# Four layers, two streams of emission: lower weights for the steps of layer 1's first two passes

## The chip, the cores and the metric

The kernel runs on one NeuronCore of a Trainium2 chip, as one program. The metric is the device time of one execution in microseconds; lower is better. The times before are those of three runs. The profile is of one further execution.

## The reference, cut to what matters

Input x has 4 images of 48 channels and 256 x 256 pixels, in float32. Four layers follow one another, each of the form x = x + layer(group_norm(x)). The group norm (`_gn`) takes mean and variance over a whole image, so a layer of an image can start only when the layer before it has finished the last row of that image. Images don't depend on one another.

```python
# layer 0: 1x1 conv to 288 channels, 3x3 depthwise, split into q, k, v;
#          8x8 patches: irfft2(rfft2(q) * rfft2(k)), normalised over channels, times v, 1x1 conv
x = x + _L0_conv_ref(_gn(x), ...)
# layer 1: 1x1 conv to 288 channels, 8x8 patches filtered in frequency,
#          3x3 depthwise, gelu(first half) * second half, 1x1 conv
x = x + _L1_conv_ref(_gn(x), ...)
# layer 2: integral image of gn(x); two 3x3 convs give a box and a scale for each pixel;
#          the integral image is sampled bilinearly at the box's four corners: (A + D - B - C) / area
x = x + _L2_conv_ref(_gn(x), ...)
# layer 3: 1x1 conv to 192, 3x3 depthwise, gelu gate, 1x1 conv, 8x8 frequency filter
x = x + _L3_conv_ref(_gn(x), ...)
```

## The kernel before

**Two streams of emission.** The program is written by two streams of Python generators, `run` (L1278). Stream a has layer 0 and layer 1 of image 0, then of image 1, 2 and 3, and after these layer 3 of images 0 to 3. Stream b has the statistics of the inputs and the filter matrices of layer 1 (`patch_weights`), and then layer 2 of images 0 to 3. Each generator emits a piece of its layer and yields a number, the weight of the step. `advance` adds it to its stream's counter `at`, and the stream with the lower counter emits next. A layer waits for the one below it of the same image: its stream's counter is then raised to the counter at which that one was done. So the weights decide only which instructions of stream b stand between which of stream a; no instruction depends on them. Every engine then takes its own instructions in the order emitted.

**The layers and their weights.** Layer 0 (L466) goes in units of two rows, 128 and 7 to drain, with two yields of 7 for each (L606, L616): 1890. Layer 1 (L659) has three passes, with pools of their own:

- Pass A (L660 to L710): 16 strips of rows are normalised (L684), multiplied by `win` (L697, 32 matmuls a strip), copied from PSUM by VectorE and ScalarE (L702, L704) and stored to `hD` in DRAM. It yields twice a strip.
- Pass B (L711 to L789): 72 groups of four channels. `fetch` loads `hg` from `hD` and the matrices `ct`, `tt` and `ht`; `filtered` (L728) applies the frequency filter, neighbours' edges are copied by DMA into `yh`, and `gated` (L741, L742) the depthwise convolution and the gate; the result goes to `gD` in DRAM. It yields once a group, 73 times.
- Pass C (L790 to L845): `gs` is loaded from `gD`, turned, projected to 48 channels, added to x and stored. It yields 5 each of 64 times.

Layer 2 (L912) begins with `sums` (L848), which builds the integral image as a table in DRAM: for both halves twelve yields of 7 and eight of 10, 328 in all. Two yields of 30 start its main part, which has 32 pieces with four steps each and a drain of four: every step has two yields of 11. A step issues 16 gathers on POOL's queue (`gather`, L1037) into `V`, which has 3 buffers; then `add` multiplies and adds the gathered corners of the step before on VectorE (L1048, L1050, L1051), `convolve` (L947), `project` (L966, L971) and `boxes` (L982 to L1029) prepare a piece two ahead, and `finish` (L1062, L1069) adds the result to x. Layer 2 weighs 3292 in all.

Layer 3 (L1134) has 128 units and 7 to drain with two yields of 4: 1080. Layers 0 and 3 share `convolve2` (L427, L435).

**Queues.** Stream a issues its DMAs from SP, stream b from POOL. Layer 2's columns A and B come through ACT's queue (L301 to L305), and `sums` stores its table from SP (L909). The two streams have PSUM banks of their own (5 for a, 2 for b) and take SBUF from opposite ends.

Of the kernel before, what the change touches and what calls it, by code (L numbers as in the profile page):

```python
# [188 lines left out]
class Net:  # L189
# [469 lines left out]
    def layer1(self, x, mr, y):  # L659
# [4 lines left out]
        with ExitStack() as ctx:  # L664
            w = ctx.enter_context(self.pool("wa", 1))
            sb = ctx.enter_context(self.pool("ba", 2))

            win = w.tile([112, 288], F32, name="win")
            mh = w.tile([112, 2], F32, name="mh")
            xns = [w.tile([112, 2, PW], F32, name=self.nm("xn")) for _ in range(2)]  # L670
            xps = [w.tile([112, 16, 128], F32, name=self.nm("xp")) for _ in range(2)]
            for t in xns:
                nc.vector.memset(t[32:64], 0.0)
            nc.vector.memset(mh[32:64], 0.0)
            for h in range(2):
                self.dma(win[64 * h : 64 * h + 48], a["L1_w_in"])
                self.dma(mh[64 * h : 64 * h + 48], mr[48 * h : 48 * h + 48])

            def normalise(s):

                for r in range(0, 8, 2):
                    xn = xns[r // 2 % 2]
                    self.load_rows(xn, x, 8 * s + r, 2, 64)
                    nc.vector.tensor_scalar(  # L684
                        xps[s % 2][:].rearrange("p b (r c) -> p r b c", c=16)[:, r : r + 2],
                        xn[:, :, 1:257].rearrange("p r (b c) -> p r b c", c=16),
                        mh[:, 0:1], mh[:, 1:2], ALU.subtract, ALU.mult,
                    )

            normalise(0)  # L690
            for s in range(NS):
                xp = xps[s % 2]
                hs = sb.tile([128, 4 * NG, 2, 16], F32, name="hs", tag="hs")
                for b in range(16):
                    for h in range(2):
                        ps = self.bank()
                        nc.tensor.matmul(  # L697
                            ps[:, :288], xp[64 * h : 64 * h + 48, b, :], win[64 * h : 64 * h + 48],
                            start=True, stop=True,
                        )  # L700
                        if h:
                            nc.vector.tensor_copy(hs[:, :, h, b], ps[:, :288])  # L702
                        else:
                            nc.scalar.copy(hs[:, :, h, b], ps[:, :288])  # L704
                    if b == 7:
                        if s + 1 < NS:
                            normalise(s + 1)
                        yield 13
                self.dma(hD[:, :, s, :], hs[:].rearrange("p (g c) h b -> p g (c h b)", c=4))
                yield 13  # L710
        with ExitStack() as ctx:  # L711
            w = ctx.enter_context(self.pool("wb", 1))
            sb = ctx.enter_context(self.pool("bb", 2))
            ys = [w.tile([128, YL], F32, name=self.nm("ys")) for _ in range(2)]
            yhs = [w.tile([NZ, YL], F32, name=self.nm("yh")) for _ in range(2)]
            hts = [w.tile([NZ, 4, 128], F32, name=self.nm("ht")) for _ in range(3)]
            for t in ys + yhs + hts:
                nc.vector.memset(t[:], 0.0)

            pick = lambda t, k, c: t[:k, Y0 + YC * c : Y0 + YC * c + 32 * YW].rearrange(  # L720
                "p (h s b) -> p s h b", h=2, b=YW
            )[:, :, :, :16]
            order = lambda t: t.rearrange("p (s h b) -> p s h b", h=2, b=16)
            todo, gt = None, None

            def filtered(c):
                ps = self.bank()
                nc.tensor.matmul(  # L728
                    ps[:].rearrange("p (s n) -> p s n", n=32), ct[:, c, :], hg[:, :, c, :], start=True, stop=True
                )  # L730
                if c % 2:
                    nc.vector.tensor_copy(pick(yt, 128, c), order(ps[:]))  # L732
                else:
                    nc.scalar.copy(pick(yt, 128, c), order(ps[:]))

            def gated(c):
                go, yo, yho, to, ho = todo
                both = []
                for q in (c, c + 2):
                    ps = self.bank()  # L740
                    nc.tensor.matmul(order(ps[:]), to[:, q, :], pick(yo, 128, q), start=True, stop=False)  # L741
                    nc.tensor.matmul(order(ps[:]), ho[:, q, :], pick(yho, NZ, q), start=False, stop=True)  # L742
                    both.append(ps)
                gl = sb.tile([128, 512], F32, name="gl", tag="gl")
                nc.scalar.activation(gl[:], both[0][:], AF.Gelu)
                nc.vector.tensor_mul(  # L746
                    gt[:, :, 2 * (go % 2) + c, :], gl[:].rearrange("p (s n) -> p s n", n=32),
                    both[1][:].rearrange("p (s n) -> p s n", n=32),
                )


            def fetch(g):
                hg = sb.tile([128, NS, 4, 32], F32, name="hg", tag="hg")
                self.dma(hg[:].rearrange("p s c n -> p s (c n)"), hD[:, g])
                ct = sb.tile([128, 4, 128], F32, name="ct", tag="ct")
                self.dma(ct[:], self.cD[g])
                tt = sb.tile([128, 4, 128], F32, name="tt", tag="tt", bufs=3)
                ht = hts[g % 3]
                tv = self.tD[4 * g : 4 * g + 4].rearrange("c (k m) -> k c m", m=128)
                self.dma(tt[:], tv[:128])  # L760
                self.dma(ht[:NH], tv[128:])
                return hg, ct, tt, ht

            fetched = {0: fetch(0)}
            for g in range(NG + 1):
                if g < NG:
                    yt = ys[g % 2]
                    if g + 1 < NG:
                        fetched[g + 1] = fetch(g + 1)
                    hg, ct, tt, ht = fetched.pop(g)  # L770
                if todo is not None and todo[0] % 2 == 0:
                    gt = sb.tile([128, NS, 4, 32], F32, name="gt", tag="gt")
                for c in range(2):
                    if g < NG:
                        filtered(2 * c)
                        filtered(2 * c + 1)
                    if todo is not None:
                        gated(c)
                if g < NG:
                    yh = yhs[g % 2]  # L780
                    n = YL - 2 * Y0
                    for k, m, p0, dp, far in AROUND:
                        self.dma(
                            yh[k : k + m, Y0 : Y0 + n], yt[p0 : p0 + (m - 1) * dp + 1 : dp, Y0 + far : Y0 + far + n]
                        )
                if todo is not None and todo[0] % 2:
                    self.dma(gD[:, :, todo[0] // 2, :], gt[:].rearrange("p s c n -> p s (c n)"))
                todo = (g, yt, yh, tt, ht)
                yield 12  # L789
        st = self.stat.tile([CP, 129, 6], F32, name=self.nm("st"), tag="st" + self.stream, bufs=1)  # L790
        with ExitStack() as ctx:
            w = ctx.enter_context(self.pool("wc", 1))
# [579 lines left out]
```

## Time and profile before

| | us |
|---|---|
| median of 3 runs | 20884.65 |
| lowest and highest | 20843.57, 20913.25 |
| profiled execution: its own time | 20882.08 |
| profiled execution: span of the instructions | 20880.3 |

| engine | busy us | share of the span |
|---|---|---|
| PE matmul | 18892.3 | 90% |
| PE weight load | 12001.4 | 57% |
| VectorE (DVE) | 10763.0 | 52% |
| ScalarE (ACT) | 5909.3 | 28% |
| GpSimd (POOL) | 8637.2 | 41% |

The DMA engines move 3440 MB at a mean of 165 GB/s. The granted clock of TensorE is 0.922 on the mean. Busy shares are averages over stages with different limits. The profile's slices and the windows by stage show where each engine is full. A count in brackets, as x1360, is the number of instructions in a stretch. Matmuls are pipelined and each of these float32 matmuls appears as two records.

### The profile page before, as it was taken

The numbers are of one execution on the slowest core, as the hardware profiler recorded it, in microseconds if no ns is written. First come the engines' busy times: TensorE is split into PE (matmuls) and PEld (weight loads), VectorE is DVE, ScalarE is ACT, GpSimd is POOL, SyncE is SP. The second block draws the span as 40 slices with busy tenths as digits, with TensorE's granted clock in tenths as the row PEclk, the third lists the DMA queues.
The fourth block names the chain that finished last, engine by engine and source line by source line (L and its number), as shares of the span: only waits on it lengthen the run. The fifth ranks groups of instructions, "written<-read, shape, count | busy, mean of one in ns | idle before, by whom it ended". The sixth has DMA issues, their size and how long they took to land.

```text
span 20880.3 us, 231985 instructions
## 1 busy us (share of the span) xinstructions
PE 18892.3 (90%) x79032; PEld 12001.4 (57%) x79032; DVE 10763.0 (52%) x21931; ACT 5909.3 (28%) x12275; POOL 8637.2 (41%) x8887
## 2 busy tenths in 40 slices
PE   7998798999878989998788899997888999999999
PEld 4565435666533346665433466654334787878888
DVE  4544322477765534677645447776554255555521
ACT  2333312344321123443311234433112211111111
POOL 1000000277754511777555216775552066666600
PEclk9899799999968999999689899996899999999999
DMA  4623886555588975555889755558897566666633
GB/s 114 135 55 82 233 217 194 137 132 134 132 235 230 241 207 139 130 134 127 233 230 240 219 133 130 133 127 229 236 239 225 137 150 151 158 152 160 151 76 74
DMA packets 2444896, 3440.27 MB, mean 165 GB/s; under 512 B 580102, under 2 KB 1997038, under 8 KB 2333179
## 3 DMA queue, kind: packets, MB, share of 16 engines
q1 hardware_dynamic: 1908216, 2084.50, 38.2%
q0 software_dynamic: 452560, 1110.45, 21.1%
q10 hardware_dynamic: 82944, 230.48, 4.4%
q8 instruction: 635, 10.40, 0.2%
q14 instruction: 541, 4.43, 0.1%
HBM read 2486.99 MB, written 802.77 MB: 158 GB/s over the span
## 4 chain that ended last, share of the span: by engine, by line
PE 65%; DMA 15%; DVE 7%; POOL 7%; issue 4%; SPq 1%; ACT 1%; DVEq 0%; ACTq 0%; POOLq 0%
PE ps L427 19%; POOL V L1037 7%; PE ps L947 6%; PE ps L728 5%; PE ps L435 4%; PE ps L741 4%; DMA ct<-cD 4%; PE ps L742 3%; PE ps L697 3%; PE ps L828 3%; DMA hD<-hs 2%; PE ps L1188 2%; DVE V L1050 2%; PE ps L815 1%; PE ps L966 1%
## 5 line engine op out<-in xcount | busy, mean ns | idle before, releaser
L1037 POOL DMA_INDIRECT V<-t,idx x8192 | 8227.0, 1004 | 4897.9 <-issue 2346.8
L427 PE MATMUL ps<-W,A 128*128 128x288 f32 (+1 forms) x24576 | 5547.3, 374 | 85.9 <-DMA A<-x 23.4
L427 PEld LDWEIGHTS ps<-W,A 128*128 128x128 f32 x24576 | 4281.6, 191 | 1226.6 <-issue 523.4
L227 POOL DMA_DIRECT2D X<-x x192 | 144.5, 757 | 4302.6 <-DMA x<-xt 3040.1
L1050 DVE TENSOR_TENSOR V<-V 128x1536 f32<-128x1536 f32 (+3 forms) x2048 | 1839.3, 900 | 19.2
L1048 DVE TENSOR_TENSOR V<-V,w 128x3072 f32<-128x3072 f32 x512 | 1713.3, 3346 | 35.9 <-DMA V<-t,idx 27.0
L728 PE MATMUL ps<-hg,ct 128*128 128x512 f32 x2304 | 1264.4, 676 | 417.5 <-DMA ct<-cD 339.5
L947 PE MATMUL ps<-A,W 112*96 112x512 f32 x3072 | 1544.9, 642 | 26.2 <-DVE xt L1069 21.5
L697 PE MATMUL ps<-win,xp 48*128 48x288 f32 x4096 | 1054.8, 594 | 547.9 <-DVE xp L684 232.4
L508 ACT COPY qkv<-ps 128x288 f32<-128x288 f32 x2048 | 769.9, 400 | 2641.1 <-PE ps L427 1258.4
L435 PE MATMUL ps<-W,B 58*128 58x288 f32 (+1 forms) x8192 | 1271.5, 391 | 26.1 <-DMA B<-x 13.8
L742 PE MATMUL ps<-yh,ht 65*128 65x512 f32 x2304 | 1163.1, 649 | 145.7 <-DMA yh<-ys 111.6
L531 DVE BATCH_NORM_STATS2 bs<-ps 128x6 f32<-128x96 f32 x2048 | 397.4, 251 | 1634.3 <-PE ps L529 1632.3
L741 PE MATMUL ps<-ys,tt 128*128 128x512 f32 x2304 | 1174.1, 632 | 27.6 <-DVE ys L732 25.7
L697 PEld LDWEIGHTS ps<-win,xp 48*128 48x128 f32 x4096 | 647.3, 259 | 924.3 <-ACT hs L704 291.9
L1168 DVE TENSOR_TENSOR gp<-gl,ps 128x192 f32<-128x192 f32 x1024 | 353.8, 351 | 1588.1 <-ACT gl L1167 1579.9
L728 PEld LDWEIGHTS ps<-hg,ct 128*128 128x128 f32 x2304 | 468.0, 211 | 1051.6 <-issue 949.1
L1167 ACT ACTIVATE gl<-ps 128x192 f32<-128x192 f32 x1024 | 332.7, 330 | 2529.4 <-PE ps L427 2245.4
L435 PEld LDWEIGHTS ps<-W,B 58*128 58x128 f32 x8192 | 762.4, 186 | 454.1 <-issue 346.4
L746 DVE TENSOR_TENSOR gt<-gl,ps 128x512 f32<-128x512 f32 x576 | 395.1, 687 | 1142.2 <-PE ps L742 1136.6
L947 PEld LDWEIGHTS ps<-A,W 112*96 112x96 f32 x3072 | 513.9, 176 | 731.4 <-issue 690.3
L742 PEld LDWEIGHTS ps<-yh,ht 65*128 65x128 f32 x2304 | 451.3, 199 | 794.3 <-issue 699.4
(186 smaller groups left out, 24654.4 us busy)
## 6 DMA issues: line engine op xcount, KB each, us to landing
hD<-hs SPq DMA_DIRECT2D x64, 4608.0 KB
hg<-hD SPq DMA_DIRECT2D x288, 1024.0 KB
gD<-gt SPq DMA_DIRECT2D x144, 1024.0 KB
gs<-gD SPq DMA_DIRECT2D x64, 2304.0 KB
V<-t,idx POOLq DMA_INDIRECT x8192
A<-x SPq DMA_DIRECT2D x512, 193.5 KB
xt<-x SPq DMA_DIRECT2D x256, 387.0 KB
A<-x ACTq DMA_DIRECT2D x512, 193.5 KB
```

Source lines behind the costliest of these rows:

```text
L427: nc.tensor.matmul(to(q, b), A[:, r + q, 128 * b + g : 128 * b + g + 128], W[:, g, :], start=b == 0 and g == 0, stop=b == 1 and g == 2,)
L435: nc.tensor.matmul(to(q, b), B[p, r // 2, 128 * b : 128 * b + 128], W[p, 3, :], start=b == 1, stop=b == 0)
L508: nc.scalar.copy(t.qkv[:, 2 * q + b, :], banks[2 * b + q][:, 0:288])
L697: nc.tensor.matmul(ps[:, :288], xp[64 * h : 64 * h + 48, b, :], win[64 * h : 64 * h + 48], start=True, stop=True,)
L728: nc.tensor.matmul(ps[:].rearrange("p (s n) -> p s n", n=32), ct[:, c, :], hg[:, :, c, :], start=True, stop=True)
L741: nc.tensor.matmul(order(ps[:]), to[:, q, :], pick(yo, 128, q), start=True, stop=False)
L742: nc.tensor.matmul(order(ps[:]), ho[:, q, :], pick(yho, NZ, q), start=False, stop=True)
L828: nc.tensor.matmul(pp[:CP, :], pr[:, q, :], got[q][:], start=q == 0, stop=q == 2)
L947: m = nc.tensor.matmul(ps[:96, :].rearrange("p (r c) -> p r c", c=256), W[: kk[g], g, :], of[: kk[g]], start=g == 0, stop=g == 3,)
L1037: nc.gpsimd.indirect_dma_start(out=V[:, k, 4 * cr : 4 * cr + 4, :].rearrange("p e c -> p (e c)"), out_offset=None, in_=table, in_offset=ba ...
L1048: self.pinned(nc.vector.tensor_mul(Vm, Vm, wm.unsqueeze(2).to_broadcast([128, 64, 48])))
L1050: nc.vector.tensor_add(V[:, :, 0:n, :], V[:, :, 0:n, :], V[:, :, n : 2 * n, :])
```

## The change

The weights of the steps of passes A and B of layer 1 are lowered: 13 to 5 at the two yields of pass A, 12 to 6 at that of pass B. Pass C and all other layers keep theirs. The weight of layer 1 of an image falls from 32 x 13 + 73 x 12 + 64 x 5 = 1612 to 32 x 5 + 73 x 6 + 64 x 5 = 918. Nothing is added to the program or taken from it; what moves is the place of layer 2's steps among those of stream a.

```diff
                     if b == 7:
                         if s + 1 < NS:
                             normalise(s + 1)
-                        yield 13
+                        yield 5
                 self.dma(hD[:, :, s, :], hs[:].rearrange("p (g c) h b -> p g (c h b)", c=4))
-                yield 13
+                yield 5
...
                 todo = (g, yt, yh, tt, ht)
-                yield 12
+                yield 6
```

## The prediction

> **What bounds the kernel now.** I read the page's slices first (busy tenths in fortieths of the span):
>
> ```profile
> PE   7998798999878989998788899997888999999999
> POOL 1000000277754511777555216775552066666600
> ```
>
> TensorE is nearly full where layer 0 runs and loose in four spells at equal distances, one for each image's layer 1. One busy share for the span says nothing, so I cut it at the first and last matmul of each stage. In this stage view the columns are the stretch, its length, busy us (count) of PE, weight loads, DVE, ACT and POOL, the granted clock, the DMA share and GB/s.
>
> ```profile
> 1983.00:2326.00 343.00, 205.88 (x1024) 158.56 (x1024) 181.67 (x315) 153.35 (x256) 0.00 (x0) 0.67 0.86 240
> 2351.00:3239.00 888.00, 823.23 (x1728) 343.16 (x1728) 202.79 (x293) 174.01 (x289) 0.00 (x0) 0.93 0.79 214
> 3254.00:3535.00 281.00, 260.90 (x1151) 150.21 (x1149) 83.52 (x183) 102.34 (x193) 0.00 (x0) 0.97 0.70 213
> 3599.00:5659.00 2060.00, 2018.83 (x8243) 1287.19 (x8242) 1322.35 (x3037) 823.32 (x1790) 1166.99 (x1159) 0.99 0.52 131
> 5699.00:6242.00 543.00, 410.41 (x1360) 225.30 (x1360) 352.37 (x617) 170.09 (x276) 296.62 (x308) 0.64 0.80 229
> 6269.00:7425.00 1156.00, 1016.97 (x2344) 432.87 (x2343) 600.25 (x888) 194.94 (x321) 609.29 (x642) 0.90 0.91 236
> 16198.00:19864.00 3666.00, 3524.22 (x21898) 2929.49 (x21898) 1874.19 (x3372) 706.88 (x1606) 2105.43 (x2157) 0.98 0.64 150
> 19864.00:20873.00 1009.00, 967.87 (x6296) 860.90 (x6295) 177.51 (x412) 186.85 (x450) 1.09 (x2) 0.97 0.36 76
> ```
>
> The first three rows are layer 1's passes A, B and C in image 0, with nothing of layer 2 beside them. Then layer 0 of image 1 beside layer 2, passes A and B of image 1 beside layer 2, layer 3 of three images beside the last layer 2, and layer 3 of the last image alone. Layer 0 and layer 3 are bound by TensorE; passes A and B move 214 to 240 GB/s with TensorE waiting, so they are bound by transfers.
>
> Layer 2's main part is 128 steps for an image, 512 in all; I call one a **V step**: 16 gathers (L1037), one multiply (L1048), four adds (L1050), its share of convolution and boxes. It weighs 22 (two yields of 11). Counting L1048 by stage tells how many lie where:
>
> ```profile
> 3599.00:5659.00 2060.00, 223.01 (x67) 0.99 0.52 131
> 5699.00:6242.00 543.00, 60.23 (x18) 0.64 0.80 229
> 6269.00:7425.00 1156.00, 130.54 (x39) 0.90 0.91 236
> 16198.00:19864.00 3666.00, 428.98 (x128) 0.98 0.64 150
> ```
>
> With the edges between stages it is 68 in layer 0, 19 in A, 39 in B and 2 in C of each image, and 128 beside layer 3. From these the **price of one V step by place**: A (543 - 343) / 19 = 10.5 us; B (1156 - 888) / 39 = 6.9 us. In layer 0, sixteen units (weight 224, so 10.2 V steps) take 187.4 us in the second half of image 0 and 242 us beside layer 2, by the starts of L579: 54.6 / 10.2 = 5.4 us. Beside layer 3, (3666 - 3 x 1009) / 128 = 5.0 us with layer 2's sums in it, about 3.8 us without. It costs little everywhere, because something else bounds each stage.
>
> Alone it would be bound by POOL's queue. The timeline of POOL (start, us, what, idle before and its releaser):
>
> ```profile
> 4566.94 0.94 POOL L1037 DMA_INDIRECT V<-t,idx  x1 [0.30 <-issue]
> 4568.18 0.97 POOL L1037 DMA_INDIRECT V<-t,idx  x1 [0.30 <-issue]
> ...
> 4571.66 1.09 POOL L227 DMA_DIRECT2D x<-xt  x2
> 4578.30 1.01 POOL L227 DMA_DIRECT2D xt<-x  x2 [5.55 <-DMA x<-xt]
> 4586.52 1.60 POOL L1037 DMA_INDIRECT V<-t,idx  x1 [7.21 <-DVE gt L1002]
> ```
>
> A gather starts 1.25 us after the one before, so 16 take 20.0 us. Once in eight V steps a strip is stored and the next loaded on the same queue, and the gathers behind stand still for up to 15 us.
>
> **What the Trainium skill says.** "Perfetto Trace Analysis", Optimization Strategy: kernels can have several regimes with different limits, and interleaving them may pay. The rows agree: a V step is cheap beside each. "DMA: Bandwidth & Descriptors", SWDGE vs HWDGE vs iDMA: what GpSimd issues has its descriptors written by software there. The trace agrees as far as POOL is occupied 0.95 us for each gather. "SBUF — State Buffer", SBUF: two separate sides: VectorE and GpSimd share a port under an exclusive lock. In the trace a gather lasts 0.95 us mostly and up to 4.3 us; 16 take 19.7 to 23.6 us, median about 21.2 beside layer 0. "TensorE: Matmul & The Clock Gate", What's actually happening: an idle array falls to half clock; A shows 0.64.
>
> **The change, part by part.** No instruction is added or removed; the weights decide the order. Layer 1 falls from 32 x 13 + 73 x 12 + 64 x 5 = 1612 to 160 + 438 + 320 = 918, layer 0 stays 1890, layer 2 stays 3292 (sums 328). Before, layers 0 and 1 of one image (3502) outlast one layer 2; now (2808) they don't, so each layer 2 ends 484 late and the delay adds up: 3 x 484 and 52 that were left over before make 1504, and layer 3 of the last image, which needs the statistics of its whole layer 2, starts that much behind layer 3 of image 2. **So not more of layer 2 lies beside layer 0**, which was covered already: in the built order on VectorE the V steps per image are 68, 63 and 65 in layer 0, 7 to 9 in A, 20 in B, 14 in C, 127 beside layer 3, and 64 with nothing of stream a between them. The sum:
>
> 1. Pass A: 57 to 23 V steps, -34 x 10.5 = -357.
> 2. Pass B: 117 to 60, -57 x 6.9 = -393. Straight lines in both, since the transfers bound them and a V step brings its own bytes. Bounds: the steps that stay might cost nothing (23 x 10.5 + 60 x 6.9 = 656 more gained), or half of the 750 may not come back.
> 3. Pass C: 6 to 42, +36 x 5 = +180. Its price isn't seen with more than two V steps; between layer 3's 3.8 and B's 6.9, 137 to 248.
> 4. Layer 0: 204 to 196, -8 x 5.4 = -43. Beside layer 3, 128 to 127: nothing.
> 5. **The tail**: 64 V steps alone. Floor 20.0 and 0.3 between steps, 64 x 20.3 = 1299; ceiling the pace beside layer 0, 242 / 10.2 = 23.8, 1523. I take 21.5, from 21.2 and a little for the strips: 1376. The others keep up: VectorE needs 3.35 + 4 x 0.90 + 0.35 (L1051) + 0.37 (L971), some 0.7 for finishing and 2.6 for boxes, 11 us; TensorE, even at A's clock, 8.3 us (1.95 us of L966 and 6.35 of L947 in the timeline at 5707). On ACT's queue the A and B loads of a step stand behind its gelu, which waits for that convolution alone. The last V step's own end was in the path before too.
> 6. Sums: image 1's and 2's sums no longer start as layer 1 ends but inside layer 0, image 3's inside layer 3. Before they filled the holes in which the next layer's weights load (3545 to 3599, 32 us of PE busy in 54; 41 in the last). TensorE, which takes its queue in order, now waits there for those weights with layer 2's matmuls queued behind: 32 + 32 + 41 = +105, between 0 and 150. The T stores on SP's queue and the X loads on POOL's go with them; layer 0's and layer 3's loads behind the former had these neighbours before.
> 7. Layer 2 restarts without a pause, three times: sums wait for the last strip's buffers, and layer 0's matmuls behind them; 20 us each by the 15 us stand above, +60, between 0 and 120.
>
> Total +928. Against the profiled execution's own 20882 that is 21810; the median of the runs is 3 us above it.
>
> **Rivals.** *Threshold, the other side*: A and B are free of layer 2's load below some density, and fall to 343 and 888 us. Then they give back 3 x (200 + 268) = 1404 in place of 750. With the rest as above 21156, still slower; it turns faster only when C's steps, the holes and the restarts cost nothing too and the tail runs at its floor: 20882 - 1404 - 43 + 1299 = 20734. The point is where all of layer 1's gain exceeds the tail. Against it: bytes don't vanish with density. *A fixed loss*: A and B stay near their length because their clock or queue is disturbed by any visit; half of the gain is lost, 22185. Against it: B moves 236 GB/s with layer 2 and 214 without, so the added bytes explain its length. *The change doesn't do what it says* in time: the tail lies beside layer 3 after all, at 3.8 us a step, 21810 - 1376 + 243 = 20677. Only if layer 3 didn't wait for group statistics of layer 2's result; it does.
>
> **How the numbers follow.** Forecast 0.77, fixed loss 0.11, threshold 0.09 (0.03 of it faster, 0.02 even), hidden tail 0.02, others 0.01. The forecast's own bounds give 21500 to 22100; taking part of threshold and fixed loss, 21380 to 22150. About 0.3% is what a measurement of this kernel can tell: faster 0.05, same 0.02, slower 0.93.
>
> **What would show it.** POOL's slices lose the pattern of three humps, stay busy through layer 1 and C, and end in a spell of some 1380 us with TensorE at 4 tenths or less and the clock down, then 1009 us of layer 3 alone. A near 416, B near 1025, C near 350 us, layer 0 near 2050. Wrong if A and B are at their lengths alone, if the tail is shorter than 1280 or longer than 1530 us, or if no stretch without layer 3's matmuls appears.

## The result and the profile after

The changed kernel takes 21536.82 us (median of 4 runs, 21522.52 to 21550.14) against 20886.03 us for the kernel before beside it: ratio 1.0313, 95% interval 1.0294 to 1.0333. It is slower by some 650 us; forecast were 21810 and a range of 21380 to 22150. Its profiled execution has a span of 21520.7 us, 640.4 more than that of before. In the runs e1 to e4 and g1 to g3 below every kernel, the one before included, has a median of 25.6 to 25.8 ms, with unchanged times where layer 2 is absent, so f1 to f4 and h1 measure five of them again.

The slices of the page, kernel after:

```profile
PE   7998798999789899987899999789899999963289
POOL 1000000376522551672236715422666326677710
PEclk9898899999779999996999999689999999986589
```

The three spells of loose TensorE in layer 1 are shorter, and at the end there is a new hole: three slices of 6, 3 and 2 tenths with POOL at 7, then layer 3 of the last image. One forecast sign did not come: POOL does not stay busy through layer 1. It keeps its humps and is busy for 131 of 407 us in pass A and 293 of 1017 in B, since fewer V steps lie there. By stage, kernel after (stretch, length, busy us and count of PE, weight loads, DVE, ACT, POOL, clock, DMA share, GB/s): passes A, B and C of image 1, layer 0 of image 2, the tail, layer 3 of image 3.

```profile
5699.00:6106.00 407.00, 295.69 (x1150) 188.06 (x1151) 245.56 (x435) 162.77 (x264) 131.29 (x138) 0.64 0.85 245
6141.00:7158.00 1017.00, 929.61 (x2064) 392.52 (x2064) 405.96 (x601) 185.42 (x307) 292.84 (x312) 0.92 0.87 228
7177.00:7517.00 340.00, 326.41 (x1424) 185.35 (x1424) 231.70 (x426) 110.46 (x208) 228.80 (x223) 0.98 0.89 270
7561.00:9613.00 2052.00, 1997.06 (x8264) 1292.50 (x8265) 1278.96 (x2956) 797.21 (x1781) 1060.39 (x1053) 0.98 0.50 126
19119.00:20524.00 1405.00, 403.10 (x1066) 191.81 (x1064) 696.45 (x1006) 40.24 (x58) 1080.31 (x1062) 0.61 0.40 101
20546.00:21514.00 968.00, 956.75 (x6272) 853.90 (x6272) 166.32 (x384) 186.12 (x448) 0.00 (x0) 0.99 0.36 74
```

Pass C of image 1 and layer 0 of image 2 in the kernel before:

```profile
7441.00:7726.00 285.00, 265.21 (x1172) 154.22 (x1170) 99.27 (x207) 102.61 (x194) 2.20 (x4) 0.96 0.72 214
7791.00:9861.00 2070.00, 2020.71 (x8246) 1289.92 (x8245) 1322.49 (x3039) 823.32 (x1790) 1170.87 (x1159) 0.99 0.52 131
```

A fell from 543 to 407, B from 1156 to 1017, C rose from 285 to 340. The tail is a stretch without any of layer 3's matmuls, TensorE busy for 403 of 1405 us. The same stretches by L1048, the multiply of a V step:

```profile
5699.00:6106.00 407.00, 23.39 (x7) 0.64 0.85 245
7561.00:9613.00 2052.00, 207.51 (x62) 0.98 0.50 126
19119.00:20524.00 1405.00, 218.01 (x65) 0.61 0.40 101
```

Seven V steps in A where 18 were, 62 in layer 0 where 67 were, 65 alone. Who waited for whom on POOL in the tail (waiting, releaser, us in total, times, longest):

```profile
POOL V L1037 <- issue: 312.6, 1026, 0.3
POOL V L1037 <- DMA V<-t,idx: 0.9, 3, 0.3
POOL V L1037 <- DVE at L1005: 0.3, 1, 0.3
```

The only idle time is the 0.3 us from one gather to the next. From 19118.5 to the end of the last gather at 20511.7 there are 1030 gathers: 64.4 V steps of 21.6 us each. POOL's queue is the bound, as forecast. The standing still at a strip is not seen here. A strip's store passes in 1.4 us, and each of the two loads, issued apart, in 0.9 us:

```profile
19403.91 0.95 POOL L1037 DMA_INDIRECT V<-t,idx  x1 [0.30 <-issue]
19404.86 1.09 POOL L227 DMA_DIRECT2D x<-xt  x2
19406.26 1.00 POOL L1037 DMA_INDIRECT V<-t,idx  x1 [0.30 <-issue]
...
19448.51 0.56 POOL L227 DMA_DIRECT2D xt<-x  x1
19449.37 0.98 POOL L1037 DMA_INDIRECT V<-t,idx  x1 [0.30 <-issue]
```

The account of the two profiled executions, by the first and last matmul of each stage (whole us), images 1 to 3 together:

| term | before | after | change | forecast |
|---|---|---|---|---|
| pass A | 1629 | 1240 | -389 | -357 |
| pass B | 3470 | 3066 | -404 | -393 |
| pass C | 854 | 1009 | +155 | +180 |
| layer 0 | 6198 | 6160 | -38 | -43 and a share of the +165 |
| between these stages | 448 | 398 | -50 | a share of the +165 |
| last convolution of layer 3's image 2 to first of image 3 | 69 | 1455 | +1386 | +1376 |
| the rest | | | -19 | 0 |
| sum | | | +641 | +928 |

### The profile page after: what moved, and what is told of

The parts are those of the page before. It is cut to its first block, busy times and chain, and to the rows that moved or that the text cites. A ratio compares the mean times of both kernels' runs of the same rounds, so it can differ in the third digit from the quotient of the medians.

```text
span 21520.7 us, 232092 instructions
## 1 busy us (share of the span) xinstructions
PE 18739.0 (87%) x79032; PEld 11986.9 (56%) x79032; DVE 10808.8 (50%) x21931; ACT 5864.6 (27%) x12237; POOL 8706.6 (40%) x8887
## 4 chain that ended last, share of the span: by engine, by line
PE 64%; DMA 13%; POOL 11%; DVE 6%; issue 5%; SPq 1%; ACT 1%; ACTq 0%; DVEq 0%; POOLq 0%
PE ps L427 20%; POOL V L1037 10%; PE ps L947 5%; PE ps L435 5%; PE ps L728 4%; PE ps L742 4%; PE ps L741 3%; PE ps L697 3%; DMA ct<-cD 3%; PE ps L1188 2%; PE ps L828 2%; DMA A<-x 1%; PE ps L885 1%; PE ps L579 1%; DMA V<-t,idx 1%
## 5 line engine op out<-in xcount | busy, mean ns | idle before, releaser
L427 PE MATMUL ps<-W,A 128*128 128x288 f32 (+1 forms) x24576 | 5552.6, 375 | 101.4 <-DMA A<-x 34.0
L427 PEld LDWEIGHTS ps<-W,A 128*128 128x128 f32 x24576 | 4288.7, 191 | 1233.8 <-issue 536.7
L1048 DVE TENSOR_TENSOR V<-V,w 128x3072 f32<-128x3072 f32 x512 | 1714.0, 3348 | 597.4 <-DMA V<-t,idx 587.1
L947 PE MATMUL ps<-A,W 112*96 112x512 f32 x3072 | 1559.9, 647 | 473.0 <-DVE xt L1069 248.9
L697 PE MATMUL ps<-win,xp 48*128 48x288 f32 x4096 | 958.1, 594 | 520.3 <-DVE xp L684 392.3
L435 PE MATMUL ps<-W,B 58*128 58x288 f32 (+1 forms) x8192 | 1260.5, 392 | 44.8 <-DVE t L519 22.8
L947 PEld LDWEIGHTS ps<-A,W 112*96 112x96 f32 x3072 | 516.6, 178 | 1179.2 <-issue 670.4
L954 ACT ACTIVATE hm<-ps,b 96x512 f32<-96x512 f32 x512 | 350.0, 684 | 2531.4 <-PE ps L947 2463.4
```

The source lines that it names most:

```text
L427: nc.tensor.matmul(to(q, b), A[:, r + q, 128 * b + g : 128 * b + g + 128], W[:, g, :], start=b == 0 and g == 0, stop=b == 1 and g == 2,)
L435: nc.tensor.matmul(to(q, b), B[p, r // 2, 128 * b : 128 * b + 128], W[p, 3, :], start=b == 1, stop=b == 0)
L697: nc.tensor.matmul(ps[:, :288], xp[64 * h : 64 * h + 48, b, :], win[64 * h : 64 * h + 48], start=True, stop=True,)
L947: m = nc.tensor.matmul(ps[:96, :].rearrange("p (r c) -> p r c", c=256), W[: kk[g], g, :], of[: kk[g]], start=g == 0, stop=g == 3,)
L1048: self.pinned(nc.vector.tensor_mul(Vm, Vm, wm.unsqueeze(2).to_broadcast([128, 64, 48])))
```

## The experiments

My theory: each V step has a price by place, and the change buys cheap relief in A and B with 64 steps at POOL's own pace; holes and restarts (items 6 and 7) cost nothing, which is why I was 277 us too high. The rival: items 6 and 7 are real, +165, and something else hid them. A third question is whether the words of the change, more of layer 2 beside layer 0, would pay if it were done.

**One pass at a time, and a version with nothing left over.** The edits to the kernel before:

```diff
# a_only          # b_only          # a7
-yield 13         -yield 12         -yield 13
+yield 5          +yield 6          +yield 7
```

and v18: the change's 5 and 6, and in layer 2's main part twice

```diff
-                    yield 11
+                    yield 9
```

The first runs of these four, e1 (`a_only`), e2 (`b_only`), e3 (`a7`) and e4 (`v18`):

> Only pass A's weights are lowered (13 to 5), pass B stays at 12. Built order: V steps 24 in A (57 before), 120 in B, 41 in C (6 before), 196 in layer 0, 5 alone at the end. Theory (prices by place, no cost of holes and restarts): A -33 x 10.5, B +3 x 6.9, C +35 x 4.1, layer 0 -8 x 5.4, tail 5 x 21.6: -117, so about 20770 us, faster than before. Rival (the prediction's items 6 and 7 are real and something else hid them): +165, about 20930 us.

> Only pass B's weight is lowered (12 to 6), pass A stays at 13. Built order: V steps 60 in B (117 before), 58 in A, 43 in C, 195 in layer 0, 30 alone at the end. Theory (prices by place, no cost of holes and restarts): B -57 x 6.9, A +1 x 10.5, C +37 x 4.1, layer 0 -9 x 5.4, tail 30 x 21.6: +368, about 21250 us. Rival (holes and restarts cost +165): about 21415 us. If the tail were not what makes the change slower, this kernel would lie at or under the kernel before.

> Pass A's weight 13 to 7, pass B 12: layers 0 and 1 weigh 3310, just more than layer 2's 3292, so nothing is left over. Built order: V steps of an image 10 in A (19), 40 in B (39), 10 in C (2), 68 in layer 0 and none alone. Theory (prices by place): 3 x (-9 x 10.5 + 6.9 + 8 x 4.1) = -165, about 20720 us, faster than both kernels. Rival (the relief of layer 1 comes only with a backlog of layer 2, or a V step costs in C what it saves in A): 20880 us.

> Weights 5 and 6 as in the change, and a V step weighs 18 in place of 22 (two yields of 9), so layer 2 weighs 2764 and nothing is left over. Built order: V steps of an image 83 in layer 0 (68), 9 in A, 24 in B, 12 in C, 98 beside the first two layers 3 and 30 beside the third, none alone. This does what the change's words say. Theory 1 (a V step costs 5.4 us in layer 0 however dense): 3 x (15 x 5.4 - 10 x 10.5 - 15 x 6.9 + 10 x 4.1) = -260, about 20625 us. Theory 2 (POOL's queue at 21.6 us a step becomes the bound of layer 0 and layer 3, since 18 of weight are 15 us of layer 0 alone): layer 0 near 2270 us an image, layer 3's first two 150 us longer, about 21100 us.

Measured: 25778.65, 25790.32, 25628.89 and 25664.02 us against 25685.76 before; ratios 1.0024 (1.0010 to 1.0039), 1.0041 (1.0030 to 1.0051), 0.9975 (0.9964 to 0.9987), 0.9994 (0.9981 to 1.0006). The forecasts in microseconds missed by 4500 to 5000, all four. Two rows by stage of e3: layer 0 of image 1 with its 67 V steps, and pass A of image 0 without any.

```profile
3605.00:6350.00 2745.00, 2193.20 (x8242) 1357.93 (x8242) 1323.91 (x3038) 821.59 (x1790) 1128.33 (x1158) 0.87 0.39 98
1987.00:2328.00 341.00, 204.29 (x1024) 158.31 (x1024) 180.21 (x315) 151.93 (x255) 0.00 (x0) 0.68 0.86 240
```

Layer 0 takes 2745 us in place of 2060, A without layer 2 its usual 341. By the same subtraction as before, a V step costs 19.6 us in A, 14.7 in B and 9.3 in C here, while the tail of e2 (30 steps alone) is 748 us, little more than the 697 of the same kernel in f3 below. A step in company comes near to what one costs alone, so moving steps changes less; that is my reading of the ratios near 1. They decide nothing about the change at the prices of its own profile. The next four runs are the same kernels at those prices; first f1, which is a7.

> The kernel of e3_a7 again (pass A's weight 7, pass B's 12, nothing left over), since in the run of e3_a7 a V step was dearer everywhere (layer 0 with 68 V steps took 2745 us in place of 2060, image 0 as before). Theory (prices by place as in the profile of before): 3 x (-9 x 10.5 + 6.9 + 8 x 4.1) = -165, about 20720 us if the kernel before takes 20885, ratio 0.992. Rival (relief of A is lost again in C): ratio 1.000.

Measured: 20749.91 against 20878.34, ratio 0.9938 (0.9922 to 0.9955). Pass A of image 1 lasts 450 us with 10 V steps, pass C 298 with 10:

```profile
5707.00:6157.00 450.00, 336.50 (x1200) 204.23 (x1200) 279.35 (x487) 166.38 (x267) 174.30 (x184) 0.63 0.84 238
7384.00:7682.00 298.00, 278.57 (x1228) 160.04 (x1228) 174.34 (x305) 104.32 (x196) 132.00 (x130) 0.96 0.82 252
```

(450 - 341) / 10 = 10.9 us in A and, with C alone at 283 in this run, (298 - 283) / 10 = 1.5 in C: what leaves A doesn't come back in C. Part of it does come back in B, which I had counted at +7 an image: over three images A falls by 281 us, C rises by 47 and B by 78. B of image 1 still has 39 multiplies of V steps, but 320 matmul records of layer 2's convolution (L947) where 264 were. So a V step's parts can lie in different stages, and a price by the count of multiplies misses that. The relief is real without a backlog, and this version beats both kernels, by a little less than the 0.992 forecast.

> The kernel of e1_a_only again. Theory (prices by place, no cost of holes and restarts): A -33 x 10.5, B +3 x 6.9, C +35 x 4.1, layer 0 -8 x 5.4, tail 5 x 21.6: -117, ratio 0.994. Rival (the prediction's items 6 and 7 are real, +165): +48, ratio 1.002.

Measured (f2, a_only): 20749.38 against 20837.68, ratio 0.9963 (0.9949 to 0.9977). The forecast of 0.994 is just outside, the rival's 1.002 well outside. A gained 403 us over three images, and the pause before layer 3's last image was 171 us (69 before), about the 108 forecast for 5 steps.

> The kernel of e2_b_only again. Theory (prices by place, no cost of holes and restarts): B -57 x 6.9, A +1 x 10.5, C +37 x 4.1, layer 0 -9 x 5.4, tail 30 x 21.6: +368, ratio 1.018. Rival (items 6 and 7 cost +165): +533, ratio 1.026. If the tail is not the cause of the loss: ratio 0.987 or less.

Measured (f3, b_only): 21113.54 against 20837.68, ratio 1.0129 (1.0112 to 1.0146), under both numbers, so again no sign of +165. It is 92 us less than the theory's +368; the spells between the stages alone are 75 us shorter than before, which the theory put at nothing. B fell to 1044, 1040 and 1032 us, a gain of 354, and yet the kernel is slower. The tail by stage:

```profile
19500.00:20147.00 647.00, 154.22 (x436) 74.41 (x434) 322.65 (x454) 16.65 (x25) 486.32 (x479) 0.59 0.37 99
```

From the last convolution of layer 3's image 2 (19463) to the first of image 3 (20160) it is 697 us, +628 for 30 V steps: 20.9 us each, forecast 648. With the change itself (64 steps, +1386) and f2 (5 steps, +102) those are three lengths of the tail at 20 to 22 us a step. The change and f2 differ in pass B's weight alone.

> The kernel of e4_v18 again: weights 5 and 6 as in the change, a V step weighs 18, nothing left over, 83 V steps in each layer 0. Theory 1 (a V step costs 5.4 us in layer 0 however dense): -260, ratio 0.988. Theory 2 (POOL's queue at 21.6 us a step becomes the bound of layers 0 and 3): about +220, ratio 1.010, with layer 0 near 2270 us.

Measured (f4, v18): 21306.69 against 20837.68, ratio 1.0229 (1.0212 to 1.0246). Theory 2, and more. Layer 0 of image 1 by stage, and the first two rows of POOL's waits in a part of it (4100 to 5800):

```profile
3586.00:5875.00 2289.00, 2122.91 (x8494) 1339.56 (x8493) 1453.75 (x3248) 833.87 (x1804) 1430.52 (x1379) 0.96 0.51 131
```

```profile
POOL V L1037 <- issue: 352.4, 1156, 0.3
POOL V L1037 <- DVE res L1051: 22.8, 5, 21.6
```

Beside layer 0 before, POOL's waits for a free `V` (DVE res L1051) were 91.1 us in 1500; here 22.8 in 1700. POOL runs almost without a pause and TensorE is busy for 2123 of 2289 us. By my estimate from the 187.4 us for 224 of weight, 18 of weight are 15 us of layer 0 alone, and POOL can't deliver a V step that often: from the first gather in layer 0 to the last it takes 22.7 us a step (23.8 before). Layer 0 was forecast at 2270. Two terms I had put too low: the next stage also starts later (66 us after layer 0, 40 before), and layer 3 takes 3834 us to its last image (3700 before). So the change's words, carried out, lose too: layer 0 had little room. The 13 further V steps, 80 by L1048 where 67 were, cost 229 us, 17.6 each and not 5.4: a price by place holds only near the density at which it was read.

**Company for what is left over.** Layer 3's steps are made heavier, so that the steps left over lie beside its first three images:

```diff
-                yield 4        # layer 3, twice
+                yield 4.4      # g1: A 5, B 12;  g2: A 5, B 11, 4.6;  g3: A 5, B 6, 5.9
```

> Pass A's weight 5, B's 12 as in f2_a_only, and layer 3's steps weigh 4.4 in place of 4, so that its first three images outlast what is left of layer 2. Built order: as f2_a_only up to layer 3; then 131 V steps beside layer 3 (126) and none alone (5). Theory (what is left over costs its time only because nothing of stream a is beside it): the 171 us between layer 3's third and fourth image fall to some 20, 5 x 3.8 come back: about 20615 us, ratio 0.989. Rival (layer 3 can't take V steps at that density, POOL's pace binds): as f2_a_only, 0.996.

> A 5, B 11, layer 3's steps 4.6. Built order: V steps 25 in A, 110 in B, 43 in C, 193 in layer 0, 141 beside layer 3, none alone. Theory (prices by place): against g1_a_only_l3 B -10 x 7.2, layer 0 -3 x 5.4, A +10.5, C +2 x 4.1, layer 3 +10 x 3.8: -31, about 20585 us, ratio 0.987. POOL needs 141 x 21.7 and some 440 for the sums, 3500 us, less than layer 3's 3640, so it doesn't bind yet. Rival (POOL binds in layer 3): 0.992 or more, with layer 3's first three images over 3750 us.

> The change's weights 5 and 6, and layer 3's steps weigh 5.9 in place of 4: no V step is left alone in the built order, 190 lie beside layer 3 (127 and 64 alone before). Theory 1 (the loss is POOL's pace: 16 gathers take 21.7 us wherever they stand): layer 3's first three images last 190 x 21.7 + 440 = 4560 us, the whole 21060 us, ratio 1.008. Theory 2 (the loss is only that the tail has no company, a V step costs 3.8 us beside layer 3): 21537 - 1405 + 64 x 3.8, about 20375 us, ratio 0.976.

Measured: 25741.78, 25638.73 and 25762.97 against 25700.17; ratios 1.0008 (0.9994 to 1.0022), 0.9981 (0.9971 to 0.9992), 1.0023 (1.0014 to 1.0032). V steps were as dear here as in e1 to e4, so nothing is decided by these three. Of them only g2 was measured again, as h1. For the change with layer 3 at 5.9 (g3) it stays open how much of the loss such company would save.

> The kernel of g2_b11_l3 again, where a V step has its usual price: A 5, B 11, layer 3's steps 4.6; 141 V steps beside layer 3 and none alone. Theory (prices by place, against f2_a_only at 0.9963: tail -150, B -10 x 7.2, layer 0 -3 x 5.4, A +10.5, C +2 x 4.1, layer 3 +15 x 3.8): ratio 0.988. Rival (POOL binds in layer 3 at that density): 0.992 or more, with layer 3's first three images over 3750 us.

Measured: 20595.91 against 20887.6, ratio 0.9859 (0.9843 to 0.9875), the fastest of all. Layer 3's first three images and the pause after them:

```profile
15826.00:19573.00 3747.00, 3571.00 (x22171) 2971.19 (x22172) 2010.94 (x3580) 722.25 (x1639) 2326.62 (x2345) 0.97 0.66 155
19573.00:19632.00 59.00, 24.59 (x98) 17.91 (x96) 9.68 (x27) 2.41 (x5) 0.00 (x0) 0.56 0.36 76
```

No tail: 59 us. The rival's number is not reached, but its direction is: 3747 us and the pause make 3806 where before had 3700, so the 13 further V steps cost 8 us each and not 3.8. Passes A and B gave 413 us against the kernel before, where the prices count 384, and the spells between the stages 69 more, which I had put at nothing.

## Why the prediction was right, point by point

**Passes A and B (items 1 and 2)** held: -389 and -404 against -357 and -393. Straight lines were near enough: a V step in A costs (413 - 342) / 7.7 = 9.3 us at the low density, and 10.9 and 10.5 at the higher ones; in B (1022 - 878) / 20 = 7.2 at 20 steps and 6.9 at 39. The threshold rival is refuted with that, and the fixed loss too. The reason given, that transfers bound both passes and a V step brings its own bytes, is argued and not shown. No run changed bytes alone; pass C moves 270 GB/s after, so 240 is no ceiling of the transfers as such; and in B TensorE is busy for 823 of 888 us alone and for 1017 of 1156 with layer 2, so 194 of the 268 us added are its own work.

**Pass C (item 3)**: +155 us for 36 more steps, 4.3 each, between the lower bound of 3.8 and the 5 taken. Against C alone in the same run, 14 steps cost 53 us, 3.8 each.

**The tail (item 5)**: 21.6 us a step, taken 21.5. POOL has no wait but its own issue. The Trainium skill, "TensorE: Matmul & The Clock Gate" (What's actually happening), states that an idle array's clock falls to half, and the tail's mean clock of 0.61 agrees. That this cost nothing is argued from two numbers: TensorE is busy for less than a third of the tail, and no gather waits for it.

**More beside layer 0**: counted beforehand as 68, 63 and 65 steps an image; by L1048 it came out as 67, 62 and 63. v18 shows why more would not have paid.

**Items 6 and 7 were the mis-sized terms.** Forecast +165; measured were -50 in the spells between the stages, -38 in layer 0 (-43 without these items) and -19 in the rest. The step that failed is the assumption that work in a hole is free, so that the hole stays as long when the work leaves. It makes most of the 287 us by which the sum was too high; the measured time lies inside the range, but near the lower end of the forecast's own bounds. The pauses between pass C and the next layer, two of before and then the same two of after, by stage:

```profile
7726.00:7791.00 65.00, 33.24 (x218) 31.72 (x219) 26.24 (x63) 9.25 (x25) 11.93 (x16) 0.75 0.64 185
11935.00:11997.00 62.00, 33.64 (x221) 32.12 (x222) 26.52 (x64) 9.25 (x25) 11.93 (x16) 0.74 0.71 198
```

```profile
7517.00:7561.00 44.00, 7.00 (x21) 4.38 (x20) 20.34 (x38) 0.26 (x1) 26.90 (x28) 0.56 0.63 154
11488.00:11531.00 43.00, 6.85 (x21) 4.38 (x20) 20.28 (x38) 0.26 (x1) 28.38 (x29) 0.59 0.64 159
```

TensorE's 33 us of sums are gone, as forecast, but so are 20 us of the pause; over three pauses 202 us became 129. The first strip of layer 0 is loaded 39 us after C's last matmul (7556 after 7517) where before it was 55 (7781 after 7726): with the sums' X loads and their normalisation (L878) out of the way, layer 0's weights and strip are ready sooner. That the loads delayed them is my reading of the order of events; it was not tried by itself. Inside layer 0 of images 2 and 3, which now hold the sums and the restart, the time fell by 17 and 31 us, 48 together, where 5 and 4 V steps fewer by L1048 make 49 at 5.4 us. So no cost of the sums or of a restart can be seen there.

Of the 287 us between forecast and account, A, B and C make 68, the tail -10, and items 6 and 7 with the rest 229.

## What to carry to other kernels

When two streams are interleaved by weights, price the moved step by its place: here 4 us in pass C, 5 beside layer 0, 7 in B, 10 in A and 21.6 alone. Such a price holds near the density at which it was read: further steps cost 17.6 us beside layer 0 (v18) and 8 beside layer 3 (h1). Relief in one stage is worth having only while the stream that was moved can still finish in company; f1 and h1 keep the relief of A and are 0.6 and 1.4% faster, the change itself pays for it with a tail. Before making one stage denser, compare its pace with the queue that feeds the other stream: 16 gathers at 1.25 us and their neighbours were the limit at 21.6 us. Work placed in a pause may lengthen that pause: the pause lost 20 us with the sums gone, though why is not shown.

## What the runs showed of the hardware

- A gather alone on its queue takes 21.6 us for 16 (1030 of them in 1393 us), even with VectorE busy for 696 of 1405 us. 1.25 us lie from one start to the next, and the rest is in gathers that last longer, up to 2.5 us, and in the strips' stores and loads.
- A strip's store on that queue takes 1.4 us and a load 0.9 us in the tail; beside layer 0 the gathers behind once stood still for 15 us.
- A V step can become far dearer with all stages without gathers unchanged: in e3, pass A of image 0 takes 341 us as in f1, the same program, but layer 0 beside layer 2 2745 us and not 2066. POOL is no longer busy there than in f1 (1128 and 1168 us). It waits for free `V` buffers (619 us from 4100 to 6300), and TensorE has waits of 103.5 us put down to issue at L427. The cause stays open.
